# Half of the maximum subtractions of 48 attention units, from GpSimd adds to accumulating transfers

## The chip, the cores and the metric

The kernel runs on one core of one Trainium2 chip. The metric is the device time of one execution in microseconds. The profile's engine names are used throughout: PE is TensorE (matmuls), PEld its weight loads, DVE is VectorE, ACT is ScalarE, POOL is GpSimd and SP is SyncE, which here only issues transfers. "L590" is line 590 of the kernel before; lines behind the edit stand four higher in the changed kernel.

## The reference

One pre-norm transformer block in float32 on x of shape [2, 1024, 1024] (2 sequences of 1024 tokens, 1024 channels), 32 heads of 32 channels, a gated feed-forward of 2752 channels. The part that matters here is the softmax of the scores.

```python
x = x + attn(layernorm(x))     # B, S, H = 2, 1024, 1024; HEADS = 32
x = x + ffn(layernorm(x))

# in attn:
scores = jnp.einsum('bhqd,bhkd->bhqk', q, k) * scale      # scale = 1 / sqrt(32)
probs = jax.nn.softmax(scores, axis=-1)                   # exp(s - max) / sum
ctx = jnp.einsum('bhqk,bhkd->bhqd', probs, v)
out = ctx @ attn_ow + attn_ob

# in ffn:
y = silu(x @ W_gate.T) * (x @ W_up.T) @ W_down.T          # F = 2752
```

## The kernel before

All matmuls are float32. The attention is cut into 64 units, each two heads of one sequence against 512 queries: 2 sequences x 2 query blocks x 16 pairs of heads. The 16 units of one sequence and one query block are a phase. While phase 0 runs, PE's other work is the projections; beside phases 1 to 3 it is what is left of the projections of the second sequence and then, block by block, the output projection and the feed-forward layers of the block whose attention is done. The fourth block's feed-forward runs alone at the end.

A unit has 8 key tiles of 128 keys. A key tile's scores are 128 x 1024 float32 (keys on the partitions; two heads x 512 queries along the row). In the code one key tile is `self.p[kt]`, and the way of a tile is this:

- `scores` (L517): PE writes the scores of two tiles to the two PSUM buffers `s`.
- `largest` (L531): DVE keeps a running elementwise maximum `top` over the 8 tiles. `keep` (L536): ACT copies the raw scores from PSUM to the SBUF tile `p`, which sets the PSUM buffer free for the next scores on PE.
- `maximum`: DVE finds the largest of each 32 queries' columns over all keys (L556, L557, L574, L575) and negates it into `neg`. SP writes it to DRAM (`d2`, 1024 floats, L580) and then reads it back into all 128 partitions as the tile `m` (L583, 512 KB).
- `less_maximum` (L590): p = p + m, one pass over 128 x 1024. In phase 0 DVE does it for tiles 3 and 7 and POOL for the others; in phases 1 to 3 POOL does it for all 8.
- `exponential` (L600): ACT replaces p by exp(scale x p).
- `add` (L613): tile kt, unless kt is 0 or 4, gets the tile before it added, so that four tiles form running sums. In phases 1 to 3 POOL adds tiles 1, 2, 5 and 6, DVE tiles 3 and 7. `differences` (L606): POOL takes the matching differences of the value rows.
- `values` (L629): PE multiplies the tiles with the values, four tiles at a time, as soon as the fourth sum is made. `finish` divides by the sum of exponentials.

The order of every engine's instructions is written by the kernel itself. An `Emitter` walks a list of steps with a planner's clock: each PE step has a cost in ns (MM4 = 855 for one float32 matmul of 512 columns), and `em.later(delay, fn)` emits a follow-up when the planner's clock has gone that far. The attention steps are paced ("beat") through the other work: a beat is one key tile, eight beats a unit. `less_maximum(kt)` of a unit is emitted LAG = 3 beats after the unit's last score beat plus kt beats, the exponential 3500 ns later, the sum 8100 to 10000 ns later. Every engine executes its own list strictly in that order and waits where an operand isn't there.

The code below holds the pieces named here. The numbers to keep: RUN = 4 (tiles in a group of PE's value products), SUMS = 4 (tiles in a running sum), 19 buffers for p, 2 for m, 3 for d2, 2 PSUM buffers for s, 8 buffers for the gate and up weights (the tag "M") and 10 for the other weights ("D"). SP issues all weight loads, one after another in one list with the transfers of `maximum`. ACT's list holds the loads of q and k (L498, L499).

Of the kernel before, what the change touches and what calls it, by code (L numbers as in the profile page):

```python
# [9 lines left out]
F32 = mybir.dt.float32  # L10
F32R = mybir.dt.float32r
AF = mybir.ActivationFunctionType
ALU = mybir.AluOpType
AX = mybir.AxisListType

P = 128
# [113 lines left out]
def preln_block_kernel(  # L130
# [14 lines left out]
    nc = tc.nc  # L145
    B, S, H = x.shape
# [23 lines left out]
    dram = ctx.enter_context(tc.tile_pool(name="dram", bufs=1, space=DRAM))  # L170
# [29 lines left out]
    def small(shape, tag, bufs, name):  # L200
        return const.tile(shape, F32, tag=tag, bufs=bufs, name=name)
# [270 lines left out]
    class Unit:  # L472
# [76 lines left out]
        def maximum(self):  # L549

            n = HD // NS
            self.m = att.tile([P, S], F32, tag="m", bufs=2, name=f"m_{self.name}")

            def half(s):
                cols = slice(s * NH, (s + 1) * NH)
                nc.vector.transpose(self.m[:, cols], self.top[:, cols])  # L556
                nc.vector.tensor_reduce(  # L557
                    part[:, s * n : (s + 1) * n],
                    self.m[:, cols].rearrange("p (b j) -> p b j", j=HD),
                    AX.X,  # L560
                    ALU.max,
                )

            for s in range(NS):
                em.later(4600.0 + 1800.0 * s, lambda s=s: half(s))
            d2 = dram.tile([S], F32, tag="d2", bufs=3, name=f"d2_{self.name}")
            neg = small([HD, HD], "neg", 1, f"neg_{self.name}")


            turned = small([HD, HPG, HD], "turned", 1, f"turned_{self.name}")  # L570

            def turn():
                for a in range(HPG):
                    nc.vector.transpose(turned[:, a, :], part[a * HD : (a + 1) * HD, :])  # L574
                nc.vector.tensor_reduce(  # L575
                    neg, turned.rearrange("b a i -> b i a"), AX.X, ALU.max, negate=True
                )

            em.later(8200.0, turn)
            em.later(12000.0, lambda: nc.sync.dma_start(d2.rearrange("(b i) -> b i", i=HD), neg))  # L580
            em.later(
                14500.0,
                lambda: nc.sync.dma_start(self.m, d2.partition_broadcast(P)),  # L583
                ("max", self.n),
            )

        def less_maximum(self, kt):
            p = self.p[kt]
            eng = nc.vector if self.phase == 0 and kt % 4 == 3 else nc.gpsimd
            eng.tensor_tensor(p, p, self.m, ALU.add)  # L590
            em.later(3500.0, lambda: self.exponential(kt))
            if kt % SUMS > 0:

                vec = self.phase == 0 or kt % RUN == RUN - 1
                delay = 8100.0 if self.phase == 0 else 10000.0 if vec else 9500.0
                eng = nc.vector if vec else nc.gpsimd
                em.later(delay, lambda: self.add(kt, eng))
# [749 lines left out]
```

## Time and profile before

| | |
|---|---|
| median of 3 runs | 3181.88 us (3179.28 to 3192.47) |
| the profiled execution | 3177.6 us |
| its span, first to last instruction | 3175.8 us |
| mean granted TensorE clock | 0.997 |
| units 16 to 63: first to last L590 | 781 to 2668 us |
| L590 on POOL, whole span | 480 instructions, 1196.6 us, 2507 ns each |
| L613 on POOL | 192 instructions, 463.5 us, 2414 ns each |
| L613 on DVE | 192 instructions, 316.6 us, 1650 ns each |
| L600 on ACT | 512 instructions, 529.0 us, 1055 ns each |
| L536 on ACT | 512 instructions, 515.4 us, 1011 ns each |
| DMA, whole span | 498 MB, 157 GB/s |

A row of the profile's groups gives the line, the engine, the operation and its tiles, how many there were, their busy time in all and the mean of one. The profile of instructions is taken in one execution, so its parts are compared with its own 3177.6 us; 3177.6 lies 4.3 us below the median of the runs. PE's busy time rests on modelled ends of matmuls. The granted clock is the share of TensorE's full clock that the chip let pass; at 0.5 a matmul takes twice as long. "DMA share" is the mean busy share of the core's 16 DMA engines.

### The profile page before, as it was taken

The page shows a single profiled execution, that of the slowest core. Times are in us where ns is not written, and L with a number is a line of the kernel's source. Part 1 is how long each engine was busy: PE and PEld are TensorE (multiplying, and loading weights), DVE is VectorE, ACT ScalarE, POOL GpSimd, SP SyncE. Part 2 cuts the span into 40 slices and gives each one's busy share as a digit, 9 for nine tenths or more (in the row PEclk, how much of TensorE's full clock was granted, in tenths as well). Part 3 has the DMA queues.
Part 4 walks back from the last instruction along what each step waited for, and adds up shares of the span by engine and source line. Part 5 has one row for each costly group of instructions (what it writes and reads, how often), then busy time and mean ns, then how long its engine had stood idle before and what let it go on. Part 6 is the DMA issues. An engine that isn't in the chain of part 4 may idle for free.

```text
span 3175.8 us, 42184 instructions
## 1 busy us (share of the span) xinstructions
PE 3132.5 (99%) x15488; PEld 1776.1 (56%) x15488; DVE 2003.7 (63%) x2813; ACT 1416.0 (45%) x1521; POOL 2000.0 (63%) x1047
## 2 busy tenths in 40 slices
PE   8999999999999999999999999999999999999999
PEld 4444444444447757563476574634766746486865
DVE  2277777776357676767677768776777675333234
ACT  2244554444457646454665564636655643010000
POOL 0267776876788777777987778779877875100000
PEclk9999999999999999999999999999999999999999
DMA  4466666655345454445344444443444544444442
GB/s 149 156 194 203 222 199 200 197 186 176 125 122 152 147 157 152 150 155 188 103 147 149 155 152 149 155 164 116 150 149 151 153 136 154 154 148 152 153 154 97
DMA packets 326686, 498.03 MB, mean 157 GB/s; under 512 B 98640, under 2 KB 115024, under 8 KB 326480
## 3 DMA queue, kind: packets, MB, share of 16 engines
q1 hardware_dynamic: 270288, 396.72, 39.3%
q10 hardware_dynamic: 56192, 98.60, 9.8%
q8 instruction: 124, 2.03, 0.3%
q14 instruction: 82, 0.67, 0.1%
HBM read 420.49 MB, written 74.71 MB: 156 GB/s over the span
## 4 chain that ended last, share of the span: by engine, by line
PE 87%; DVE 7%; ACT 2%; POOL 2%; DMA 1%; issue 1%; ACTq 0%; SPq 0%; DVEq 0%; POOLq 0%
PE p L912 31%; PE pq L378 14%; PE pd L1068 13%; PE acc L629 8%; PE s L517 8%; PE pvv L440 6%; PE po L764 3%; DVE top L531 1%; PE pd L988 1%; DVE h L1043 1%; PE pg L956 1%; DVE p L613 1%; DVE x L1081 1%; POOL p L590 1%; POOL x L756 0%
## 5 line engine op out<-in xcount | busy, mean ns | idle before, releaser
L590 POOL TENSOR_TENSOR p<-p,m 128x1024 f32<-128x1024 f32 x480 | 1196.6, 2507 | 27.3 <-DMA m<-d 25.8
L536 ACT COPY p<-s 128x1024 f32<-128x1024 f32 x512 | 515.4, 1011 | 792.7 <-DVE top L531 660.5
L613 POOL TENSOR_TENSOR p<-p,p 128x1024 f32<-128x1024 f32 x192 | 463.5, 2414 | 355.0 <-ACT p L600 332.8
L531 DVE TENSOR_TENSOR top<-s,top 128x1024 f32<-128x1024 f32 x384 | 468.9, 1221 | 294.5 <-PE s L517 276.7
L600 ACT ACTIVATE p<-p 128x1024 f32<-128x1024 f32 x512 | 529.0, 1055 | 243.7 <-POOL p L590 188.9
L912 PE MATMUL p<-sum,m 128*128 128x256 f32 x2688 | 611.2, 382 | 1.5 <-DVE gate L926 1.1
L912 PEld LDWEIGHTS p<-sum,m 128*128 128x128 f32 x2688 | 504.7, 190 | 105.5 <-issue 32.7
L912 PE MATMUL p<-xn2T,m 128*128 128x256 f32 x2016 | 462.7, 381 | 1.7 <-DVE x L776 1.7
L378 PE MATMUL pq<-xnT,wqk 128*128 128x512 f32 x1024 | 457.7, 600 | 0.0
L1068 PE MATMUL pd<-wp,h 128*128 128x512 f32 x960 | 428.6, 599 | 3.8 <-DVE x L1081 3.7
L912 PEld LDWEIGHTS p<-xn2T,m 128*128 128x128 f32 x2016 | 379.2, 190 | 81.1 <-issue 25.0
L613 DVE TENSOR_TENSOR p<-p,p 128x1024 f32<-128x1024 f32 x192 | 316.6, 1650 | 48.1 <-ACT p L600 42.3
L378 PEld LDWEIGHTS pq<-xnT,wqk 128*128 128x128 f32 x1024 | 190.3, 191 | 249.5 <-issue 247.8
L1068 PEld LDWEIGHTS pd<-wp,h 128*128 128x128 f32 x960 | 179.3, 190 | 237.5 <-issue 214.8
L517 PE MATMUL s<-q,k 32*128 32x512 f32 x2048 | 301.5, 641 | 4.3 <-ACT p L536 4.3
L1178 POOL TENSOR_TENSOR raw<-raw 128x512 f32<-128x512 f32 x62 | 97.1, 1567 | 262.9 <-DMA raw<-in_w_gu 170.4
L629 PE MATMUL acc<-p,vals 128*32 128x256 f32 x4096 | 248.2, 382 | 3.3 <-DVE p L613 3.2
L440 PE MATMUL pvv<-wv,xnT 128*128 128x512 f32 x512 | 230.5, 600 | 0.3 <-ACT xnT L274 0.3
L764 PE MATMUL po<-wo,ctx 128*128 128x512 f32 x512 | 229.1, 601 | 0.0
L629 PEld LDWEIGHTS acc<-p,vals 128*32 128x32 f32 x4096 | 119.6, 109 | 166.5 <-issue 86.4
L1081 DVE TENSOR_TENSOR x<-pd,x 128x512 f32<-128x512 f32 x216 | 143.0, 683 | 103.7 <-PE pd L1068 103.6
L975 POOL MEMSET h<- 64x512 f32 x4 | 2.1, 517 | 287.9 <-PE pd L1068 287.9
(93 smaller groups left out, 2517.9 us busy)
## 6 DMA issues: line engine op xcount, KB each, us to landing
m<-dws SPq DMA_DIRECT2D x336, 256.0 KB
m<-in_w_gu SPq DMA_DIRECT2D x252, 256.0 KB
wp<-ddn SPq DMA_DIRECT2D x160, 256.0 KB
m<-d SPq DMA_DIRECT2D x64, 512.0 KB
wp<-in_w_dn SPq DMA_DIRECT2D x120, 256.0 KB
raw<-in_w_gu ACTq DMA_DIRECT2D x84, 256.0 KB
dws<-raw ACTq DMA_DIRECT2D x84, 256.0 KB
x<-in_x SPq DMA_DIRECT2D x32, 512.0 KB
```

The source lines that it names most:

```text
L378: nc.tensor.matmul(ps, wqk[b, g, w, hk][:, k, :], xnT[b, s][:, kc, :], start=(kc == 0), stop=(kc == KC - 1),)
L440: nc.tensor.matmul(st["ps"], xnT[b, t // TB][:, kc, (t % TB) * P : (t % TB + 1) * P], st["w"][kc], start=(kc == 0), stop=(kc == KC - 1),)
L517: nc.tensor.matmul(ps[a][:, h * NH : (h + 1) * NH], self.k[rows, i * P : (i + 1) * P], self.q[rows, :], start=True, stop=True,)
L531: nc.vector.tensor_tensor(self.top, s, self.p[0] if kt == 1 else self.top, ALU.max)
L536: nc.scalar.copy(self.p[kt], s)
L590: eng.tensor_tensor(p, p, self.m, ALU.add)
L600: nc.scalar.activation(self.p[kt], self.p[kt], AF.Exp, scale=SCALE)
L613: eng.tensor_tensor(self.p[kt], self.p[kt], self.p[kt - 1], ALU.add)
L629: nc.tensor.matmul(self.acc[j * HD : (j + 1) * HD, c : c + NQ], w(h), self.p[kt][:, q0 : q0 + NQ], start=start, stop=stop, skip_group_chec ...
L764: nc.tensor.matmul(st["ps"], ctxT[b, blk][:, g, t * P : (t + 1) * P], st["w"][hf, g], start=(g == 0), stop=(g == G - 1),)
L912: nc.tensor.matmul(ps, mats[c, n][:, kc, :], rhs, start=(kc == 0), stop=(kc == hk - 1),)
L1068: nc.tensor.matmul(st["pd"], lefts[n](pi)[j // 2][:, j % 2, t * P : (t + 1) * P], st["wp", pi, n, j], start=(j == 0), stop=(j == len(parts ...
```

## The change

In phases 1 to 3 the subtractions of tiles 1, 3, 5 and 7 of every unit are no longer additions on POOL. For each of these tiles POOL issues a transfer that reads the 1024 floats of d2 from DRAM for all 128 partitions and accumulates them onto the tile in SBUF. The transfers are issued where `less_maximum` of an even tile is emitted: those of tiles 1 and 3 just ahead of the addition of tile 0, that of tile 5 ahead of the addition of tile 2, that of tile 7 ahead of the addition of tile 4. That is one beat ahead of its old place for tile 1 and three beats for the others. The exponential and the sum of each tile are emitted when they were. In phase 0 nothing changes.

```diff
-            d2 = dram.tile([S], F32, tag="d2", bufs=3, name=f"d2_{self.name}")
+            d2 = self.d2 = dram.tile([S], F32, tag="d2", bufs=3, name=f"d2_{self.name}")
...
         def less_maximum(self, kt):
             p = self.p[kt]
-            eng = nc.vector if self.phase == 0 and kt % 4 == 3 else nc.gpsimd
-            eng.tensor_tensor(p, p, self.m, ALU.add)
+            moved = () if self.phase == 0 else (1, 3, 5, 7)
+            for k in {0: moved[:2], 2: moved[2:3], 4: moved[3:]}.get(kt, ()):
+                nc.gpsimd.dma_start(self.p[k], self.d2.partition_broadcast(P), accum_op=ALU.add)
+            if kt not in moved:
+                eng = nc.vector if self.phase == 0 and kt % 4 == 3 else nc.gpsimd
+                eng.tensor_tensor(p, p, self.m, ALU.add)
             em.later(3500.0, lambda: self.exponential(kt))
```

192 of the 480 additions on POOL are replaced so; 288 stay. On PE, DVE, ACT and SP the instructions and their order are as before.

## The prediction

> **What bounds the kernel now.** I read the page first, engines and slices, to see who is full.
>
> ```profile
> span 3175.8 us, 42184 instructions
> PE 3132.5 (99%) x15488; PEld 1776.1 (56%) x15488; DVE 2003.7 (63%) x2813; ACT 1416.0 (45%) x1521; POOL 2000.0 (63%) x1047
> DMA  4466666655345454445344444443444544444442
> ```
>
> PE is busy 99% of the span; POOL, which the change relieves, 63%. A time can fall only by what PE still waits. The change works only in units 16 to 63, whose subtractions run from 781 to 2668 us, so I cut the span there (columns: length, then busy us of PE, PEld, DVE, ACT, POOL with counts, granted clock, DMA share, GB/s).
>
> ```profile
> 0.00:820.00 820.00, 803.07 (x3438) 343.97 (x3442) 524.16 (x600) 354.58 (x386) 505.61 (x290) 0.99 0.58 186
> 820.00:2680.00 1860.00, 1837.95 (x10271) 1102.35 (x10261) 1300.34 (x1876) 1029.17 (x1077) 1478.93 (x745) 1.00 0.47 147
> ```
>
> PE idles 1860.0 - 1837.95 = 22.05 us here, POOL 381 us, and the DMA engines stand at 0.47. Third view, what ended PE's waits in the same stretch:
>
> ```profile
> PE pt_f L266 <- ACT xn L257: 5.2, 3, 2.5
> PE s L517 <- ACT p L536: 4.3, 4, 1.8
> PE pd L1068 <- DVE x L1081: 4.3, 5, 1.9
> PE acc L629 <- DVE p L613: 3.2, 2, 1.8
> PE p L912 <- DVE x L776: 1.7, 1, 1.7
> ```
>
> No line names POOL or a DMA. The clock adds to it: in three stretches of 5 us, each beginning at one of the longer waits, the granted clock is 0.66 to 0.67:
>
> ```profile
> 1454.00:1459.00 5.00, 4.74 (x7) 1.98 (x8) 5.00 (x8) 1.77 (x2) 0.00 (x0) 0.67 0.82 263
> 1519.00:1524.00 5.00, 4.93 (x21) 2.06 (x22) 4.79 (x9) 0.29 (x2) 5.00 (x4) 0.66 0.23 52
> 2209.00:2214.00 5.00, 4.49 (x20) 2.56 (x21) 0.93 (x2) 4.70 (x6) 5.00 (x4) 0.66 0.01 5
> ```
>
> That loses 5 x 0.34 = 1.7 us each, 5.0 in all. So **27 us**, 0.85% of the time, is all that this stretch can give back.
>
> Last, how POOL enters a PE wait, in the order of time (start, length, engine, line; in brackets the idle before and what ended it):
>
> ```profile
> 1513.26 2.35 POOL L613 TENSOR_TENSOR p<-p,p 128x1024 f32<-128x1024 f32 x1
> ...
> 1515.56 2.37 POOL L590 TENSOR_TENSOR p<-p,m 128x1024 f32<-128x1024 f32 x1
> 1515.64 3.37 DVE L613 TENSOR_TENSOR p<-p,p 128x1024 f32<-128x1024 f32 x1 [2.85 <-POOL p L613]
> ...
> 1519.07 0.64 PE L629 MATMUL acc<-p,vals 128*32 128x256 f32 x8 [1.76 <-DVE p L613]
> ```
>
> DVE's sum of two SBUF tiles takes 3.37 us while POOL subtracts beside it; the same operation took 1.21 us at 1573.16, where POOL was idle. Sums stretched in this way (this one, L613 at 3.38 and 2.89, L1043 at 2.6) stand in the chains ahead of most of the s, pd and acc waits.
>
> **The change, part by part.** The order of instructions on PE, DVE, ACT and SP stays; on POOL 192 of the 384 subtractions of these units become DMA issues at or ahead of their place. Four exponentials a unit (tiles 1, 3, 5, 7) now wait for a transfer instead of for POOL.
>
> *Removed:* 192 x 2.47 us (mean of L590 in this stretch) = 474 us of POOL. POOL is off the path, so that is no time by itself.
>
> *Added on POOL:* 192 issues. No POOL issue is in the trace. Lower bound: SP's issue of a transfer of this size, m<-d, 0.33 us; upper bound: the tensor pass it replaces, 2.47, since only addresses are handled. Neither is near in kind; I take the middle, 1.4: 192 x 1.4 = 269 us. POOL goes from 1479 to 1274 of 1860 us (0.80 to 0.69); at the bounds to 1068 or to 1479 as before. [...] An issue waits for d2, which POOL's next instruction, tile 0's subtraction, waits for already through m; behind it queue that subtraction and the sums L613, then the exponentials on ACT.
>
> *Added on the DMA engines:* 192 transfers of 128 rows of 4096 bytes, 8 rows for each of 16 engines. A 4096-byte packet of the existing loads took 159 ns at the median, so one pass is 8 x 0.159 = 1.27 us of all engines. An accumulation also reads its target. Lower bound one pass (1.27); upper bound two reads at the packets' 99th percentile in this stretch, 552 ns: 8.8 us. I take two passes, 2.54, nearest to the undisturbed rows: 192 x 2.54 = 488 us of 1860, +0.26: the share goes from 0.47 to 0.73 (0.60 at the low end, over 1 at the high end). [...]
>
> *Weights under that load:* PE never waits on a weight DMA now. A gate/up weight tile is issued 11.6 us before its first use at the least, and the 512 KB broadcast m<-d takes 3.2 to 5.5 us from its issue to the last of its 4096-byte packets in these 48 units (median 3.7, first packet at 0.97). A 256 KB tile delayed by two whole accumulations (5.1 us) still lands in time, so I charge nothing; without that cover each late tile would cost its delay on PE.
>
> *The new wait.* Landing time: issue 1.4 + 0.97 to the first packet + twice the moving time 2 x (3.7 - 0.97) = 7.9 us. The lead, from the start of tile 0's subtraction on POOL to the start of tile 1's exponential on ACT, over the 48 units: 5.2 at the least, 11.4 at the median, 8 units under 7.9. Tiles 3, 5, 7: at least 14. So tile 1 is late in 8 units by 1.2 us on average, 9.3 us in all. Queued behind that exponential on ACT are the copies L536, which free the two score buffers for PE. ACT is busy 55% of the stretch, so I let one quarter through: **+2.3 us**.
>
> *What PE gets back.* Two-input POOL passes (L590 and L613) fill 922 + 457 = 1379 us of the stretch; without 474 they fill 905, a third less. I take a third of the waits whose chains hold a stretched DVE sum (4.3 + 4.3 + 3.2 = 11.8): **-3.9**, and a third of the clock's 5.0: **-1.7**. The pt_f and xn2T waits (5.2 + 1.7) come from the norm's ACT and DVE steps and stay. Bounds: 0 and all 27.
>
> *Sum:* +2.3 - 3.9 - 1.7 = -3.3 us. The profiled execution took 3177.6 (span 3175.8), so 3174.3; the median of the runs lies 4.3 higher, so **3178.6** to compare.
>
> **Rivals.** 0.5%, 16 us, is about what a measurement of this kernel can tell from no change.
>
> 1. *No change within 0.5%* (forecast): what POOL loses was hidden, what the DMA engines gain is hidden. 3172 to 3190. Chance 0.49.
> 2. *PE's waits go almost all*: three quarters of 27 = -20, 3162. For it: the stretched sums in nearly every chain. Against it: 6.9 us have no POOL in them, and a third of the POOL passes is not all. Chance 0.13.
> 3. *Late landings block ACT* (slower): the accumulation moves at a quarter of a copy's rate instead of half. Then it lands after 1.4 + 0.97 + 4 x 2.73 = 13.3 us, past tile 1's median lead of 11.4, and tile 3, issued right behind, past its 20.5; the engines' share becomes 0.47 + 0.52 = 0.99. Exponentials hold up L536, L536 holds up the scores on PE. It decides from about 11.4 us per landing; at about 1 us of PE per unit, 48 units, +48: 3230. For it: the wait d<-neg on a 4 KB transfer already reaches 8.3 us in a crowded place. Against it: 0.53 of the engines is free. Chance 0.24.
> 4. *The issue holds POOL longer than the pass it replaces*: POOL's 381 idle us over 192 issues are 2.0 us, so POOL is full at 4.45 us an issue; at 4 us it is at 0.95, and every sum and exponential in order behind it is later: half a microsecond or so on PE per unit, +30: 3212. Chance 0.14.
>
> That the edit does nothing is excluded by the order of the instructions.
>
> **How the numbers follow.** Likeliest is the first, 3179. Its own range is 3172 to 3190. The whole range goes down to 3160 (most of case 2) and up to 3235 (case 4 and the middle of case 3), leaving out the far half of case 3 and a little of 2, under 0.2. Faster by over 0.5%: 0.13. Within: 0.49. Slower: 0.24 + 0.14 = 0.38.
>
> **What would show it.** Right: L590 x288 on POOL, POOL near 1800 us, DMA share near 0.7 in the middle slices, PE's waits on no DMA, DVE's L613 and L1043 below their 1.65 and 1.3 to 1.9 us means, exponentials of odd tiles waiting on the transfer only at tile 1 and seldom. Wrong: PE waits on weight tiles (the load does not hide), ACT idle before L600 for hundreds of us because of DMA (case 3), or long gaps on POOL at the issues (case 4).

## The result, and the profile after

The changed kernel took 3222.47 us (median of 4 runs, 3217.84 to 3224.43) beside 3181.1 for the kernel before on the same chip: a ratio of 1.0120 with a 95% interval of [1.0094, 1.0147]. It is slower by 41 us. The profiled execution took 3224.43, its span 3222.7, 46.9 us more than before.

From the page of the changed kernel, its engines, its DMA slices and two groups:

```profile
span 3222.7 us, 42235 instructions
PE 3150.1 (98%) x15488; PEld 1781.4 (55%) x15488; DVE 2024.9 (63%) x2813; ACT 1413.9 (44%) x1521; POOL 1685.5 (52%) x1047
DMA  4566666556667777788777786877777876444552
...
L594 POOL TENSOR_TENSOR p<-p,m 128x1024 f32<-128x1024 f32 x288 | 806.2, 2815 | 23.1 <-DMA m<-d 19.1
...
L591 POOL DMA_DIRECT2D p<-d x192 | 198.4, 1108 | 17.1 <-DMA d<-neg 12.1
```

POOL's busy time fell by 314 us (2000.0 to 1685.5), and the DMA slices rose to 7 and 8 tenths. Two numbers are odd. 288 subtractions are left, but the mean of one rose from 2507 to 2815 ns. And the busy times of POOL's groups add up to 1859 us, 174 more than its busy time (24 more in the kernel before): records of POOL overlap, and the busy time counts an overlap once. The stretch of units 16 to 63 in the table by stage:

```profile
820.00:2720.00 1900.00, 1850.64 (x10267) 1105.55 (x10266) 1318.10 (x1874) 1025.50 (x1076) 1174.72 (x745) 0.99 0.75 196
```

PE's idle time there is 1900.0 - 1850.64 = 49.4 us; it was 22.05. So 27 of the 47 us are new waits. What ended them:

```profile
PE s L517 <- ACT p L536: 12.4, 9, 3.4
PE acc L633 <- DVE p L617: 9.3, 3, 6.0
PE p L916 <- ACT gate L928: 6.2, 4, 3.6
PE pd L1072 <- DVE x L1085: 5.3, 6, 1.6
```

No DMA is among them, and among ACT's waits in this stretch none is for one of the new transfers. Most of the rest is the clock. In the changed kernel's clock record after 700 us four stretches of 6.83 us and five of 3.41 stand at 0.50, in the kernel before three of 3.41. In the stretch at 922.6 the 128x512 matmuls start 854 ns apart, ahead of it and behind it 429. Half of these stretches would be lost if PE worked all the time, (27.3 + 17.1 - 10.2) / 2 = 17 us more than before; with PE's busy time in these stretches alone it is 15.5 us more (20.6 against 5.1). Each stretch begins within a wait of PE or at most 2.6 us behind one. One of them (columns: length, busy us of PE, PEld, DVE, ACT and POOL with counts, granted clock, DMA share, GB/s):

```profile
922.60:929.40 6.80, 4.92 (x20) 2.10 (x21) 6.59 (x9) 2.81 (x3) 6.72 (x4) 0.50 0.37 77
```

It begins at 922.6, so I looked at the timeline of the changed kernel just ahead of it:

```profile
908.79 1.78 POOL L591 DMA_DIRECT2D p<-d  x2
909.62 14.81 DVE L617 TENSOR_TENSOR p<-p,p 128x1024 f32<-128x1024 f32 x1
909.93 3.02 POOL L594 TENSOR_TENSOR p<-p,m 128x1024 f32<-128x1024 f32 x1
912.24 5.59 POOL L760 TENSOR_TENSOR x<-x,bo 128x512 f32<-128x512 f32 x4
917.12 1.54 POOL L591 DMA_DIRECT2D p<-d  x1
917.74 3.30 POOL L594 TENSOR_TENSOR p<-p,m 128x1024 f32<-128x1024 f32 x1
920.05 6.61 POOL L617 TENSOR_TENSOR p<-p,p 128x1024 f32<-128x1024 f32 x2
...
924.48 1.08 PE L633 MATMUL acc<-p,vals 128*32 128x256 f32 x8 [6.02 <-DVE p L617]
```

A sum on DVE that takes 1.2 us by itself takes **14.81 us**. It begins while POOL issues, outlasts a third issue at 917.12, and ends at 924.43. That is 1.09 us behind the end (923.34) of the first of the two sums L617; the second has to wait for the first and begins 0.08 us behind that end. At the six earlier ends of POOL's passes within the sum, POOL's next instruction had begun 0.70 to 0.99 us ahead of the end. PE waits 6.02 us for the sum. Note POOL's records: L594 starts at 909.93 and lasts 3.02, to 912.95, but the next pass starts at 912.24. Between 820 and 2700 us 120 pairs of consecutive passes overlap by over 0.15 us, by 0.99 at most; in the kernel before, none does by over 0.1. The very same sum of the very same unit in the kernel before:

```profile
906.93 2.35 POOL L590 TENSOR_TENSOR p<-p,m 128x1024 f32<-128x1024 f32 x1
907.33 3.03 DVE L613 TENSOR_TENSOR p<-p,p 128x1024 f32<-128x1024 f32 x1
909.24 3.47 POOL L756 TENSOR_TENSOR x<-x,bo 128x512 f32<-128x512 f32 x2
```

There DVE is held for the rest of one POOL pass: the sum ends 1.08 us behind the pass's end, though POOL goes straight on. Between 820 and 2700 us 21 of the 95 sums of that kernel take over 1.65 us, and each ends 1.08 to 1.09 us behind the end of a POOL pass. That this is not one accident is seen in the view of single lines, which gives the least, median and largest duration in ns; first the changed kernel (820 to 2720 us; L946 and L1047 are DVE's steps of the feed-forward layers):

```profile
L617 DVE TENSOR_TENSOR p<-p,p x94: 1172/1215/14809, 834.0 to 2710.4; 128x1024 f32<-128x1024 f32 x94
...
L946 DVE TENSOR_TENSOR h<-gate,up x63: 691/694/7316, 1004.3 to 2716.4; 128x512 f32<-128x512 f32 x63
...
L1047 DVE TENSOR_TENSOR s<-h x14: 680/948/9599, 1134.4 to 2604.1; 128x512 f32<-128x512 f32 x14
...
L531 DVE TENSOR_TENSOR top<-s,top x276: 1202/1225/1227, 822.0 to 2662.1; 128x1024 f32<-128x1024 f32 x138
...
L594 POOL TENSOR_TENSOR p<-p,m x188: 2337/2699/3379, 825.1 to 2701.2; 128x1024 f32<-128x1024 f32 x188
```

and the kernel before in the same columns (L1043 from 820 to 2680 us):

```profile
L613 DVE TENSOR_TENSOR p<-p,p x95: 1202/1216/3379, 831.7 to 2683.1; 128x1024 f32<-128x1024 f32 x95
...
L942 DVE TENSOR_TENSOR h<-gate,up x63: 691/1043/5491, 990.6 to 2669.6; 128x512 f32<-128x512 f32 x63
...
L1043 DVE TENSOR_TENSOR s<-h x14: 896/2116/2865, 1114.7 to 2556.1; 128x512 f32<-128x512 f32 x14
```

The median of DVE's sum did not move; its largest went from 3.4 to 14.8 us. The medians of the other two fell, their largest rose. L531, equally large but with one operand in PSUM, never exceeds 1.227 us, and no other kind of DVE's work in this stretch lasts over 0.02 us longer than its median. Only operations with both inputs in SBUF are held here. Counted over all such operations of DVE between 820 and 2700 us (worked out from the rows of the trace): before 229, of which one is over 4 us (5.5); after 221, of which **21 are over 4 us, 136 us together**: one sum L617, nine of L946, eight of L1047 and three others. Each of the 21 ends 0.56 us (those of 128x512) or 1.09 us (the two of 128x1024) behind the end of a POOL pass at which POOL's next instruction hadn't begun yet; at every end of a pass before it, within the same operation, that had begun 0.30 to 0.99 us ahead. PE's long waits go with them. Seven times in this stretch PE stands still for over 2 us, 23.7 us together, and each of the seven ends at most 4 us behind the end of such an operation; before, one wait is over 2 us (2.5), and no long operation is near it.

### The profile page after: what moved, and what is told of

Its sections match the earlier page's. It is cut to its first block, busy times and chain, and to the rows that moved or that the text cites. A ratio compares the mean times of both kernels' runs of the same rounds, so it can differ in the third digit from the quotient of the medians.

```text
span 3222.7 us, 42235 instructions
## 1 busy us (share of the span) xinstructions
PE 3150.1 (98%) x15488; PEld 1781.4 (55%) x15488; DVE 2024.9 (63%) x2813; ACT 1413.9 (44%) x1521; POOL 1685.5 (52%) x1047
## 4 chain that ended last, share of the span: by engine, by line
PE 86%; DVE 9%; DMA 2%; ACT 2%; issue 1%; POOL 0%; ACTq 0%; SPq 0%; DVEq 0%; POOLq 0%
PE p L916 30%; PE pq L378 14%; PE pd L1072 12%; PE acc L633 8%; PE s L517 7%; PE pvv L440 6%; PE po L768 6%; DVE h L1047 2%; DVE top L531 2%; PE pd L992 1%; DVE p L617 1%; DVE h L946 1%; DVE x L1085 1%; PE pg L960 1%; DMA d<-neg 1%
## 5 line engine op out<-in xcount | busy, mean ns | idle before, releaser
L617 POOL TENSOR_TENSOR p<-p,p 128x1024 f32<-128x1024 f32 x192 | 493.1, 2568 | 685.7 <-ACT p L604 672.6
L594 POOL TENSOR_TENSOR p<-p,m 128x1024 f32<-128x1024 f32 x288 | 806.2, 2815 | 23.1 <-DMA m<-d 19.1
L531 DVE TENSOR_TENSOR top<-s,top 128x1024 f32<-128x1024 f32 x384 | 469.1, 1222 | 295.9 <-PE s L517 278.1
L617 DVE TENSOR_TENSOR p<-p,p 128x1024 f32<-128x1024 f32 x192 | 303.7, 1583 | 50.6 <-ACT p L604 44.8
L517 PE MATMUL s<-q,k 32*128 32x512 f32 x2048 | 305.7, 646 | 12.5 <-ACT p L536 12.4
L591 POOL DMA_DIRECT2D p<-d x192 | 198.4, 1108 | 17.1 <-DMA d<-neg 12.1
```

The lines of the kernel that those rows point to most:

```text
L517: nc.tensor.matmul(ps[a][:, h * NH : (h + 1) * NH], self.k[rows, i * P : (i + 1) * P], self.q[rows, :], start=True, stop=True,)
L531: nc.vector.tensor_tensor(self.top, s, self.p[0] if kt == 1 else self.top, ALU.max)
L617: eng.tensor_tensor(self.p[kt], self.p[kt], self.p[kt - 1], ALU.add)
```

## The experiments

*Theory S*: behind a POOL-issued transfer POOL's passes run into each other, as in the records above, and DVE's two-SBUF-input operations get no turn until POOL next waits for its own work. What an issue would leave behind inside POOL is a guess; no record shows it. *Theory L*: the load of the new transfers on the DMA engines and on SBUF makes the loss. Ratios are to the kernel before on the same chip, with 95% intervals. "Long" operations are DVE's two-SBUF-input ones over 4 us between 820 and 2700 us. Lines shift by the few lines of each edit.

### Waiting for POOL's own end behind the issues

The changed kernel, and behind each group of issues two memsets of one column:

```diff
+    mark = const.tile([P, 1], F32, tag="mark", name="mark")
...
-            for k in {0: moved[:2], 2: moved[2:3], 4: moved[3:]}.get(kt, ()):
+            issued = {0: moved[:2], 2: moved[2:3], 4: moved[3:]}.get(kt, ())
+            for k in issued:
                 nc.gpsimd.dma_start(self.p[k], self.d2.partition_broadcast(P), accum_op=ALU.add)
+            for _ in range(2 if issued else 0):
+                nc.gpsimd.memset(mark, 0.0)
```

Both write the same column, so the second waits until the first has ended: in each of the 144 groups it begins 0.06 us behind that end.

> The changed kernel, with two small POOL memsets of one column behind each group of issues; the second waits until the first is done on all of POOL, so that nothing that the issue left unfinished runs into the next pass. Theory S (the issue leaves parts of POOL behind, the following passes run into each other, and DVE's sums of two SBUF tiles cannot start until the run ends): 3172 to 3192 us, DVE's two-input operations over 4 us in the stretch 820 to 2700 fall from 21 to 3 at most, and POOL's L590-type passes return to 2.35 us. Theory L (the 100 MB more on the DMA engines make the chain of the maximum and the loads late): 3215 to 3230, since the transfers are all still there.

Measured: 3168.28 us, 0.9951 [0.9932, 0.9970], 4 us under the range of S. The same transfers are still there, and now the change gains. None of 233 operations is long; the longest is 3.1 us. The same place in the timeline of this kernel:

```profile
905.64 1.78 POOL L593 DMA_DIRECT2D p<-d  x2
906.75 0.93 POOL L595 MEMSET mark<- 128x1 f32 x2
907.69 2.34 POOL L598 TENSOR_TENSOR p<-p,m 128x1024 f32<-128x1024 f32 x1
908.21 2.90 DVE L621 TENSOR_TENSOR p<-p,p 128x1024 f32<-128x1024 f32 x1
910.00 5.92 POOL L764 TENSOR_TENSOR x<-x,bo 128x512 f32<-128x512 f32 x4
```

The pass behind the memsets is back at 2.34 us, the next starts at its end (in 820 to 2700 us no two passes overlap by over 0.15 us), and DVE's sum (2.90 us) waits for one pass again. That speaks for S, and against L, since nothing was taken from the load: the DMA share is 0.78.

### One memset, so no wait

As above, with `range(1 if issued else 0)`.

> The changed kernel with ONE one-column memset behind each group of issues, so nothing waits for POOL's own end. [...] Rival (any instruction between the issue and the pass mends it, by its length or its place): near the run with two, 3166 to 3172.

S expected no gain from it, 3210 to 3228 with 15 to 25 long operations. Measured: 3221.65, 1.0126 [1.0107, 1.0146], with 19 long operations, 122 us together. The place once more:

```profile
907.29 0.78 POOL L595 MEMSET mark<- 128x1 f32 x1
907.35 3.02 POOL L598 TENSOR_TENSOR p<-p,m 128x1024 f32<-128x1024 f32 x1
909.14 12.76 DVE L621 TENSOR_TENSOR p<-p,p 128x1024 f32<-128x1024 f32 x1
```

A one-column memset took 0.78 us, the next pass began 0.06 us after the memset's start and runs 3.02 us, and DVE is held again. So it is not an instruction between issue and pass that mends it, but the wait for POOL's own end. (Two memsets on different columns, without the wait, were not run.)

### The pairs of memsets alone

The kernel before with the pairs at the same places and no issues (the loop of memsets above, without the transfers).

> The kernel before with the pairs of one-column memsets at the places of the issues, and no issue or transfer. Control for the run with the pairs that stood at 0.9951. [...] Rival (the pairs gain by themselves, by making a gap between POOL passes in which DVE gets through): about 3168, and the gain of the other run is not the change's.

S expected no change, 3175 to 3185. Measured: 3182.69, 1.0004 [0.9995, 1.0013]; no long operation (largest 4.0). The pairs gain nothing by themselves and cost nothing: the gain of the first experiment belongs to the moved tiles.

### The load alone, twice

The kernel before and plain transfers of 512 KB from d2 to DRAM scratch, issued by SP ahead of the subtraction; `range(2)` in the first, 384 of them:

```diff
+            if self.phase > 0:
+                for k in {0: (1, 3), 2: (5,), 4: (7,)}.get(kt, ()):
+                    for i in range(2):
+                        spare = dram.tile([P, S], F32, tag="spare", bufs=8, name=f"spare_{self.name}_{k}_{i}")
+                        nc.sync.dma_start(spare, self.d2.partition_broadcast(P))
             eng.tensor_tensor(p, p, self.m, ALU.add)
```

> The kernel before, with 384 more 512 KB transfers of d2 (two for each moved tile, issued by SP at the same place, into spare DRAM tiles that nobody reads), which is the engine time of the accumulations without any issue on POOL; all subtractions stay on POOL. Theory S: 3178 to 3192 us, no DVE two-input operation over 6 us. Theory L: 3210 to 3230, PE idle in the stretch near 45 us.

Measured: 3226.08, 1.0139 [1.0114, 1.0164]. By the time alone this is L's number, and S's is missed. But the load came out heavier than meant, with a DMA share of 0.89 in 820 to 2720 us against 0.75, and PE now waits for weights too:

```profile
PE p L917 <- DMA m<-dws: 5.8, 3, 2.9
```

Weights come late here, which the changed kernel never shows (14.7 us of such waits, of PE's 51.7 idle us in 820 to 2720; what lengthened the others was not followed up), and only one of DVE's operations is long. The run doesn't decide, so the load was set to the changed kernel's: one transfer instead of two at each place, and one more at tile 6, 240 in all.

> The kernel before with a DMA load and nothing else: 240 plain transfers of 512 KB, issued by SP from d2 into DRAM scratch; by the earlier load run (384 of them took the DMA share from 0.47 to 0.90) this should bring the share to about 0.74, where the changed kernel stands at 0.75. POOL's work is that of before. Theory S (DVE is kept waiting behind POOL's issues; the load itself is hidden): 3178 to 3190, ratio below 1.003, at most 3 of DVE's two-SBUF-input operations over 4 us. Theory L (the DMA load makes the loss): 3215 to 3225. In between, some of the loss belongs to the load.

Measured: 3185.15, 1.0009 [0.9995, 1.0024], at a share of 0.74; one long operation, as before. At the size that the change brings, the load on the DMA engines is hidden; L falls. These transfers end in DRAM; that accumulating onto SBUF is hidden as well is shown by the first experiment, which has all of it.

### The issue alone

The kernel before, with all its subtractions, and 192 POOL-issued transfers of 128 x 4 bytes into a spare SBUF tile:

```diff
+    spare = const.tile([P, 8], F32, tag="spare", name="spare")
...
+            if self.phase > 0:
+                for k in {0: (1, 3), 2: (5,), 4: (7,)}.get(kt, ()):
+                    nc.gpsimd.dma_start(spare[:, k : k + 1], self.d2[:1].partition_broadcast(P))
             eng.tensor_tensor(p, p, self.m, ALU.add)
```

> The kernel before, with 192 POOL-issued transfers of 128 rows of 4 bytes at the changed kernel's places, into a spare tile that nobody reads; all subtractions stay on POOL, the DMA engines get next to no load. Theory S: 3205 to 3270 us, POOL passes overlapping behind the issues and at least 20 DVE two-input operations over 4 us. Theory L: 3178 to 3192, DVE as before (1 over 4 us).

Measured: 3444.46, 1.0823 [1.0795, 1.0851], far past every number written down. 34 operations are long, 337 us together. PE's waits and the same sum in this kernel:

```profile
PE acc L633 <- DVE p L617: 85.1, 9, 18.6
```

```profile
905.26 1.09 POOL L593 DMA_DIRECT2D spare<-d  x2
906.36 2.36 POOL L594 TENSOR_TENSOR p<-p,m 128x1024 f32<-128x1024 f32 x1
906.86 27.37 DVE L617 TENSOR_TENSOR p<-p,p 128x1024 f32<-128x1024 f32 x1
```

Behind issues of 0.55 us and 512 bytes each (two here, one more at 915.87 and one at 925.63) a sum is held for 27 us. The DMA share is 0.43, below that of before, so no load is at work. POOL's passes keep 2.36 us here, and none overlaps the next by over 0.1 us, against what S expected: longer and overlapping passes are a companion of the loss in the changed kernel, not its condition. Why it is worse than the change: POOL still does all subtractions, so its stretches without a pause are longer, 17.7 us in the mean against 11.0 in the changed kernel (from the ends and starts of POOL's rows in 820 to 2700 us, pauses over 0.15 us counted). That explanation of the size is argued, not tested. Long stretches alone do nothing: before, their mean is 16.9 us.

### The issue alone, with the wait

The same with the pair of memsets behind each group.

> The run with 192 tiny POOL-issued transfers on top of the kernel before (3444), and behind each group of issues two one-column memsets on POOL, the second of which waits for the end of the first. [...]

S expected 3180 to 3200 and at most 3 long operations, its rival, that an issue costs by itself, 3300 or more. Measured: 3207.56, 1.0079 [1.0063, 1.0095]: 237 of the 264 us are gone with two tiny memsets. The place, with DVE's sum at its undisturbed length:

```profile
907.20 1.08 POOL L595 DMA_DIRECT2D spare<-d  x2
908.08 1.22 DVE L621 TENSOR_TENSOR p<-p,p 128x1024 f32<-128x1024 f32 x1
908.27 0.27 POOL L597 MEMSET mark<- 128x1 f32 x2
```

In this place the sum began before the pass did, so the row alone proves little; that the long operations fell from 34 to two does. The time stays 8 us above the expected range, with two long operations (5.4 and 12.4 us) and three more half-clock stretches than the kernel before between 700 us and the end. POOL has more to do here than in the kernel before (1578 against 1470 us in 820 to 2660). Which of these makes the remaining 27 us was not settled.

### All four issues in one group

The changed kernel with the four issues of a unit together ahead of the `differences` (three passes, each overwriting rows that the one before reads):

```diff
+        def issue(self):
+            for k in (1, 3, 5, 7):
+                nc.gpsimd.dma_start(self.p[k], self.d2.partition_broadcast(P), accum_op=ALU.add)
...
-            for k in {0: moved[:2], 2: moved[2:3], 4: moved[3:]}.get(kt, ()):
-                nc.gpsimd.dma_start(self.p[k], self.d2.partition_broadcast(P), accum_op=ALU.add)
...
+                if kt == 0 and units[k].phase > 0:
+                    q.add(units[k].issue, needs=("max", k))
```

> The changed kernel, with all four transfers of a unit issued in one group ahead of the value differences L606, whose second and third passes wait for the first on all of POOL; nothing else added. Theory S: 3168 to 3195 us, DVE two-input operations over 4 us at most 5. Theory L: 3215 to 3240, the same bytes and four transfers at once.

Measured: 3239.97, 1.0176 [1.0152, 1.0201]. The number was missed, but no operation is long (largest 3.4 us): I take it that the three dependent passes behind the issues do what the memsets do (in the changed kernel the second and third of them begin 0.08 us behind the end of the one before). The loss is another one. POOL's own waits in this kernel, and one of them:

```profile
POOL p L589 <- issue: 103.4, 23, 6.9
```

```profile
1523.99 2.68 POOL L589 DMA_DIRECT2D p<-d  x3 [2.50 <-DMA d<-neg]
1531.51 0.88 POOL L589 DMA_DIRECT2D p<-d  x1 [4.83 <-issue]
```

The fourth issue in a row stands still for 4.83 us, and everything behind it on POOL with it. The 23 waits of that row are only a part: the waits of the other units are put down to PE, but they end with the landings of the transfers like these. It is the same in all 48 units: the fourth issue waits 2.5 to 6.9 us, 217 us together, and begins 0.25 to 0.31 us after the first of the four has landed; here that one landed at 1531.20. So POOL began no issue in this kernel while three of its transfers were on the way; at the starts of the changed kernel's 192 issues at most two were. What runs out at three is not shown, and neither is how much of the loss these waits make.

### How many tiles

With the pairs of memsets, two tiles of a unit (3 and 7), six (all but 0 and 4, issued ahead of tiles 0 to 4), and the four again. By S the gain is what POOL's fewer two-input passes free for DVE, so two tiles were expected to have half the gain of four: 0.997 to 0.998, 3171 to 3176, at a DMA share of 0.62. Its rival, that the gain comes from something else or is nearly all had with the first tiles, stood at 3167 to 3169. The edit for two tiles:

```diff
-            moved = () if self.phase == 0 else (1, 3, 5, 7)
-            issued = {0: moved[:2], 2: moved[2:3], 4: moved[3:]}.get(kt, ())
+            moved = () if self.phase == 0 else (3, 7)
+            issued = {0: moved[:1], 4: moved[1:]}.get(kt, ())
```

> The version with the pairs of memsets, but only tiles 3 and 7 of a unit moved (96 transfers, one issue ahead of tile 0 and one ahead of tile 4). [...]

> The version with four tiles moved and the pairs of memsets again, in five rounds beside the other two, to narrow the interval [0.9932, 0.997] of its first run: 0.9945 to 0.9955 expected, 3163 to 3169, with at most 18 of DVE's two-SBUF-input operations over 2.5 us and none over 4.

> The version with the pairs of memsets, with six tiles of a unit moved (1, 2, 3, 5, 6 and 7; 288 transfers, POOL subtracts only tiles 0 and 4). Theory S alone would give half as much gain again: 0.9927, 3157. The DMA share would be 0.47 + 6/4 x 0.31 = 0.93, and the run with a share of 0.90 had PE waiting on weights and stood at 1.014. So expected: the load decides, PE waits on weight DMAs, 3180 to 3230. If it comes under 3167 the load is still hidden at 0.93 when the transfers are POOL's.

| tiles moved | time | ratio | DMA share, 820 to 2660 | DVE operations over 2.5 us |
|---|---|---|---|---|
| 2 | 3169.79 | 0.9956 [0.9942, 0.9971] | 0.64 | 30 |
| 4 | 3164.61 | 0.9940 [0.9921, 0.9959] | 0.78 | 15 |
| 6 | 3182.31 | 0.9993 [0.9980, 1.0006] | 0.91 | 12 |

The kernel before has 47 in the last column at a share of 0.47. Two tiles give more than the half that I expected: 3169.79 lies under the range of S and 1 us over that of its rival, so what makes the gain, freer sums on DVE or something else such as the earlier exponentials, is not shown. The intervals of two and four overlap, so which of them is better isn't shown either. With six tiles DVE is freer still, but the gain is gone, as expected from the load, and the first of PE's waits is new:

```profile
PE po L772 <- DMA wo<-in_w_o: 7.4, 4, 2.6
```

Here too issues waited for the oldest of three transfers to land, 14 of them and 20.6 us in all. Four tiles and the pairs of memsets beat both kernels in two separate runs (0.9951 and 0.9940). The table by stage of the second:

```profile
820.00:2660.00 1840.00, 1824.37 (x10269) 1099.33 (x10270) 1212.84 (x1874) 1025.51 (x1075) 1198.59 (x1027) 1.00 0.78 202
```

PE idles 15.6 us there instead of 22.05, and after 700 us the clock record has one stretch at 0.50 instead of three, 1.7 us lost instead of 5.1. That is 10 of the 15 us between the two profiled executions (3177.6 and 3162.4); where the rest comes from was not settled.

## Why the prediction was wrong

**Right, step by step.** *Added on POOL*: 1.4 us an issue, measured 1.1 (1108 ns in the mean; 0.90 at the median). *Added on the DMA engines*: 2.54 us of all engines, measured 8 packets of 328 ns = 2.6; share 0.73, measured 0.75. *Landing time*: 7.9 us, measured 7.9 at the median (4.9 to 12.1). *Weights under that load*: nothing charged, and PE waits on no DMA; the matched load alone gave 1.0009. Rival 3 (late landings) did not come: an accumulation moved at half the rate of a copy (328 against 159 ns a packet at the median), not at a quarter. *The new wait*, +2.3, did not come either: no wait of ACT in the changed kernel is for a new transfer. Two readings were off without entering the sum: the longest wait d<-neg is 8.0 us, not 8.3, and the 99th percentile of the 4096-byte packets in the stretch 541 ns, not 552.

**The step that failed is *What PE gets back***, -3.9 and -1.7 us. It took POOL's cost to DVE as a matter of how many passes POOL makes: a third fewer, so a third of the waits. The direction of that step is not wrong, since with the pairs of memsets the same moves brought 0.9940: PE's idle time fell by 6.4 us and the lost clock by 3.4. (The time, 3165, is near the 3162 of rival 2, but 15.6 of the 22 us of waits are still there, so they did not go almost all.) But the step assumed that DVE would be held by one pass at a time, as in nearly all rows of before (the sums 3.4 us at most), and so it put the cost of an issue to DVE at nothing. Behind an issue that did not hold: the sum of 14.81 us outlasted six ends of passes. In place of -5.6 the changed kernel showed +27 us of waits and some +16 of clock. The clock term has a lesson of its own: I scaled it with the old waits, but it grew with new ones of a few us.

**Rival 4** named the right instruction and the wrong price. It asked how long the issue holds POOL, and decided at 4 us. The issue takes 1.1, and with 0.55 us in the run with tiny transfers it cost most of all. What an issue does to the engine that works beside POOL was asked nowhere, though the prediction's own timeline showed DVE waiting beside POOL. The range up to 3235 held the time by luck: by the width that rivals 3 and 4 gave it, not by their reasons.

**What would show it** was half blind. I named DVE's means as the sign. L613 below 1.65 us came true, 1.58 (303.7 us over 192), in the slower kernel: fewer sums met a POOL pass (in the stretch 88 of 94 took at most 1.65 us, before 74 of 95), and one met the stall of 14.8. L1043 gave the warning: two of its three kinds went up instead of down, from 1.60 to 1.97 and from 1.91 to 2.31 us. POOL near 1800 us was missed too (1685.5), by the overlaps, which the busy time counts once.

**Cause, and what stays open.** Shown: issues alone, with next to no bytes, make a loss of this kind (1.0823); the load of this size doesn't (1.0009); a wait for POOL's own end behind the issue takes the loss away (0.9951), and a memset without the wait doesn't (1.0126); only operations of DVE with two SBUF inputs are held, and the 21 long ones of the changed kernel until POOL itself paused. Inferred: that something of POOL runs on behind an issue, so that DVE finds no turn between two passes. In the rows of before a sum is held by one pass (3.03 us beside a pass of 2.35); 14.81 us don't fit a single pass, of which the longest subtraction in the stretch took 3.38. POOL's overlapping records fit the inference: 120 pairs of passes overlap by over 0.15 us in the changed kernel, 121 with one memset, none with two. But no record here shows what a pass does inside POOL, and in the run with tiny transfers, where the sums were held longest, the overlaps stayed under 0.1 us, so it is not shown. One row of before hints that an issue is not the only way into this: its single long operation (L942 at 2033.27, 5.49 us) stands through a POOL memset of 64 of the 128 partitions and through the two passes behind it. One case proves nothing.

## What to carry to other kernels

Where POOL issues a transfer and then works on SBUF without a pause, look at the longest durations of DVE's operations with two SBUF inputs, not at their means; a pair of dependent one-column memsets behind the issue (0.63 us of POOL in the mean of 144 pairs) took the stalls away here. Price a moved step also by what it does to the engine beside it, and prove a suspected price by the smallest kernel that has it alone, as the run with 512-byte transfers does. Look at the waits of a fourth POOL transfer (here 512 KB each) with three on the way: here it waited 2.5 to 6.9 us, until one had landed, and POOL's work behind it waited too. A time that matches a theory is no proof of it: the heavy load run had the loss of the changed kernel to 4 us, with one long operation instead of 21.

## What the runs showed that I had not expected

With issues of 0.55 us on POOL one operation of DVE lasted 27.4 us instead of 1.2. In the changed kernel the clock fell to 0.50 for 3.41 or 6.83 us at PE waits of 0.9 to 6 us, half of which, up to 1.7 or 3.4 us, was lost again; other waits of the same length passed without it. POOL began no issue with three of its transfers on the way: 48 issues in one kernel and 14 in another waited, up to 6.9 us, until one of the three had landed. And with the DMA engines busy 0.78 of 1.8 ms, no weight was late by more than 1.4 us.
